# Series of unread matmuls behind the last output of a convolution network

## The chip, the cores and the metric

The kernel runs on one core of one Trainium2 chip. The metric is the device time of one execution in microseconds, the median of the runs shown. A profile of one execution gives the span from its first to its last instruction.

## The reference

The input is `x`, four images of 32 x 32 pixels with 16 channels, float32. Four residual layers follow one another: `x = x + layer(group_norm(x))`. Layers 0, 1 and 3 have the form

```python
first   = einsum('ijyx,byxc->bijc', M, x)
shifted = conv3x3(x, kernels)            # 32*32*16 output channels: one 3x3 filter per (i, j, f)
diff    = relu(x[:, None, None] - shifted)
second  = einsum('ijyx,bijyxc->bijc', W, diff)
layer   = first - second
```

so for every output pixel (i, j) and filter f the whole image is convolved with a filter of its own, subtracted, clipped and summed with weights W. Layer 2 pools over intervals and has three small dense steps with maxima. The result has the shape of `x`.

## The kernel before, in words

**Tiling.** The four images are two groups of two (`GB` = 2). Six phases run over (layer, group) for the three convolution layers; each phase has 8 tiles `t` of 128 output pixels, and each tile 32 steps (filter f of 16, image b of 2). That makes 1536 steps. A step makes, for 128 output pixels, the clipped and weighted sum over one image of 1024 pixels for one filter.

**A step on TensorE.** The image is cut into two halves of 512 pixels. The 9 taps x 16 channels of the contraction are spread over slots of 64 partitions: `iy`, `iz`, `iyz` have two slots each (`s` = 0, 1), `im9` one. To keep precision, each operand is split into an upper and a lower part; `WU`, `WL`, `WD` are the three weight parts (in one tile, `parts`, [128, 2, 3, 4, 128]), `W9` the weights of the ninth tap. `products` (line 593) issues, for each pair (weights, moving operand), two matmuls: one with partitions 0 to 63, one with 64 to 127, each into its own PSUM bank of a pair of banks, `half = h ^ b`. A step has 7 such pairs: 4 in `first_part` (line 610: `WU` x `iy` and `WL` x `iz`), then ScalarE scales the PSUM pair (line 630), then 3 in `second_part` (line 633: `WD` x `iyz` and `W9` x `im9`). The moving operand has `NH` = 512 columns, but the last matmul of the bank `half` = 1 has `LAST` = 480. All of them are recorded under line 601. At the end of a step VectorE reads the PSUM pair, clips it and multiplies with W, summing (line 646).

**Order of the work.** `conv_layer` (line 673) runs by hand: each step issues its `first_part`, then the `second_part` of the step before it, so that TensorE has work while ScalarE scales. Between steps, generators feed in small pieces of other work: the weights' preparation (`prep_parts`, line 213), the next phase's normalisation and images, the interval layer (matmuls of lines 521 and 534) and the first terms (matmuls of line 398: 256 moving columns, 32 weight columns, plain float32, which the profile shows as two records for each matmul). PSUM has four buffers, each a pair of banks (`bank_pair`, line 81), taken in rotation; a step's buffer is free when VectorE has read it.

**The end.** After the last phase the remaining `second_part` is issued (line 871): 3 pairs of matmuls, then VectorE's sum and the addition to `X` (line 664). The last line, 872, sends the last tile of `X` out by SyncE's queue. Nothing stands behind it.

Of the kernel before, what the change touches and what calls it, by code (L numbers as in the profile page):

```python
# [15 lines left out]
P = 128  # L16
B, H, C = 4, 32, 16
NG = 2
GB = B // NG
# [8 lines left out]
NH = HI * H  # L28
RUN = (HI - 1) * HP + H
LAST = (HI - 1) * H  # L30
ROWS = P // H
FU = 4
NU = C // FU
# [9 lines left out]
def net_kernel(ctx: ExitStack, tc: tile.TileContext, x, xq, xi, convs, iv_w, iv_b, out):  # L43
# [26 lines left out]
    nc = tc.nc  # L70
# [13 lines left out]
    def bank(name):  # L84
        return bank_pair(name)[:, 0]
# [3 lines left out]
    n_chunks = len(phases) * NT  # L89
# [12 lines left out]
    raws, units, chunks = {}, {}, {}  # L102

    def load_raw(u):
        if u < n_chunks * NU:
            n = u // NU
            raws[u] = wpool.tile([P, 3, FU, P], F32, tag="raw", bufs=RAWS, name=f"raw_{u}")
            nc.sync.dma_start(raws[u], convs[phases[n // NT][1]][2][n % NT, u % NU])
# [13 lines left out]
    iy = [const.tile([P, 2, GB, NH], F32R, name=f"iy{g}") for g in range(NG)]  # L122
    iz = [const.tile([P, 2, GB, NH], F32R, name=f"iz{g}") for g in range(NG)]
    iyz = [const.tile([P, 2, GB, NH], F32R, name=f"iyz{g}") for g in range(NG)]
    im9 = [const.tile([P, GB, NH], F32R, name=f"im9{g}") for g in range(NG)]
# [35 lines left out]
    pick = (ident[:, 4 * C : 5 * C], ident[:, :C])  # L161
# [9 lines left out]
    def halve(dst, src, mask):  # L171
        nc.scalar.activation(dst, src, AF.Copy, scale=mask[:, 1:2])  # L172
# [19 lines left out]
    def upper(src, n, name):  # L192

        t = work.tile([P, 2, NH], F32, tag="upper", bufs=2, name=f"upper_{name}")[:, :n]
        t = t.rearrange("p s (y x) -> p s y x", x=src.shape[3])
        nc.vector.tensor_scalar(  # L196
            t.bitcast(I32), src.bitcast(I32), HIGH, None, op0=ALU.bitwise_and
        )
        return t.rearrange("p s y x -> p s (y x)")

    def prep(u, at=0, to=FU, eng=nc.gpsimd):

        if u >= n_chunks * NU:
            return
        f0 = u % NU * FU
        for s in range(2 if u < PLAIN else 1):
            eng.tensor_tensor(  # L207
                raws[u][:, s, at:to], raws[u][:, s, at:to],
                pick[s][:, f0 + at : f0 + to].unsqueeze(2).to_broadcast([P, to - at, P]),
                ALU.subtract,  # L210
            )

    def prep_parts():

        for u in range(PLAIN, n_chunks * NU):
            parts = wpool.tile([P, 2, 3, FU, P], F32R, tag="parts", bufs=AHEAD + 1, name=f"parts_{u}")
            W9 = wpool.tile([P, FU, P], F32R, tag="W9", bufs=AHEAD + 1, name=f"W9_{u}")  # L220
            units[u] = [parts[:, :, k] for k in range(3)] + [W9]
            src = raws.pop(u)
            w8 = src[:, 0].rearrange("p f k -> p (f k)")
            WU, WL, WD = (parts[:, 0, k].rearrange("p f k -> p (f k)") for k in range(3))
            high = upper(src[:, 0:1], 1, f"w{u}")[:, 0]
            yield (IDLE,)
            halve(W9, src[:, 1], low_w)
            yield ()
            nc.scalar.activation(WD, high, AF.Copy, scale=-EPS)  # L229
            nc.gpsimd.tensor_tensor(WL, w8, high, ALU.subtract)  # L230
            nc.gpsimd.tensor_tensor(W9, W9.bitcast(F32), src[:, 2], ALU.add)  # L231
            yield ()
            nc.scalar.copy(WU, high)  # L233
            nc.gpsimd.tensor_tensor(WD, WD.bitcast(F32), WL.bitcast(F32), ALU.add)  # L234
            yield ()
            prep(u + 1)
            yield (IDLE,)
            yield (IDLE, CALM)
            for h in range(2):
                nc.sync.dma_start(  # L240
                    parts[64 * h : 64 * h + 64, 1].bitcast(F32),
                    parts[64 - 64 * h : 128 - 64 * h, 0].bitcast(F32),
                )
            load_raw(u + RAWS)
            yield (IDLE, CALM)
            yield (IDLE, CALM)
# [168 lines left out]
    wv = const.tile([P, 7, C], F32, name="wv")  # L415
# [308 lines left out]
    pairs = const.tile([P, C // 2], F32, name="pairs")  # L724
# [41 lines left out]
    def first_stats(src, name):  # L766

        ps = bank(f"ps_{name}")
        by_batch = work.tile([P, GB], F32, tag="by_batch", name=f"by_batch_{name}")
        nc.vector.tensor_scalar_mul(by_batch, own, src)  # L770
        nc.tensor.matmul(  # L771
            ps[:, :GB], lhsT=to_rows.rearrange("p k g s -> p (k g s)"), rhs=by_batch,
            start=True, stop=True,
        )
        return ps[:, :GB]

    nc.vector.tensor_reduce(s1, XQ, axis=AX.X, op=ALU.add)
    ps = bank("ps_own")
# [3 lines left out]
    m = first_stats(s1, "m0")  # L782
# [57 lines left out]
    def rest_of_start():  # L840
# [25 lines left out]
        yield from group_norm(0, "c00", xns[0], 4)  # L866

    parts = prep_parts()
    for phase in range(len(phases)):
        conv_layer(phase, behind(phase))  # L870
    second_part(*open_steps.pop(0))
    nc.sync.dma_start(out[1][:, NT - 1], X[1][:, NT - 1])


# [74 lines left out]
```

## Time and profile before

| | us |
|---|---|
| median of 2 runs (2525.25 and 2526.16) | 2525.7 |
| profiled execution, its own time | 2525.65 |
| its span | 2523.9 |
| TensorE busy | 2509.2, 21906 records |
| line 646 on VectorE | 1879.7, 1536 of 1.224 |
| line 630 on ScalarE | 1531.8, 1520 of 1.008 |
| start of the last pair of matmuls | 2519.22 |
| issue of the last DMA (line 872) | 2521.19 |
| that DMA from issue to landing | 1.4 |

How to read it: PE is TensorE's matmuls, PEld its weight loads, which are recorded apart and run beside matmuls. A record such as `64*128 64x512` is 64 rows of weights with 128 columns, and 64 partitions of 512 moving columns. In the timeline neighbouring records of one kind are merged; the first number is the start, the second the length of the merged piece, `x4` the number of records. A matmul's record lasts from its start to its modelled end, longer than the time after which the next can start.

### The profile page before, as it was taken

How to read it: one execution, taken by the hardware profiler on the slowest of the kernel's cores; microseconds unless marked ns; L12 is line 12 of the kernel's file. 1: busy time of each engine (PE TensorE's matmuls, PEld its weight loads, DVE VectorE, ACT ScalarE, POOL GpSimd, SP SyncE). 2: the span in 40 equal slices, each digit the busy share in tenths (PEclk: the TensorE clock that was granted, in tenths of full speed). 3: DMA queues.
4: the chain of work that ended last, by engine and by line, in shares of the span. 5: the costliest groups of instructions: out<-in, count | busy, mean ns of one | idle time of the engine just before them, and what ended most of it. 6: DMA issues, size and time to landing. Idle time of an engine off the chain costs nothing.

```text
span 2523.9 us, 56662 instructions
## 1 busy us (share of the span) xinstructions
PE 2509.2 (99%) x21906; PEld 2186.7 (87%) x21906; DVE 2080.3 (82%) x3621; ACT 1890.2 (75%) x2181; POOL 1103.6 (44%) x990
## 2 busy tenths in 40 slices
PE   8999999999999999999999999999999999999999
PEld 5888888888888888888888889988999898888887
DVE  8888777888777887777788988888888887778877
ACT  3777777787777777777777777787777777777776
POOL 3445333454333335333345555454646344333332
PEclk9999999999999999999999999999999999999999
DMA  5556444464444654444454444554444466354442
GB/s 173 180 151 169 120 135 137 117 168 139 131 139 131 200 163 118 139 131 133 135 143 134 131 119 136 144 159 128 124 135 137 130 170 201 111 143 134 134 135 53
DMA packets 81182, 353.80 MB, mean 140 GB/s; under 512 B 18448, under 2 KB 20368, under 8 KB 80144
## 3 DMA queue, kind: packets, MB, share of 16 engines
q1 hardware_dynamic: 79920, 349.57, 49.2%
q8 instruction: 172, 2.82, 0.5%
q14 instruction: 98, 0.80, 0.1%
q10 hardware_dynamic: 864, 0.58, 0.1%
q0 software_dynamic: 128, 0.02, 0.0%
HBM read 199.19 MB, written 0.98 MB: 79 GB/s over the span
## 4 chain that ended last, share of the span: by engine, by line
PE 99%; ACT 0%; DVE 0%; issue 0%; POOL 0%; DVEq 0%; ACTq 0%; POOLq 0%
PE pc L601 97%; PE pf L398 1%; ACT pc L630 0%; DVE junk L646 0%; PE ps_l L521 0%; PE ps_r L534 0%; ACT L326 0%; ACT L564 0%; DVE raw L817 0%; PE ps_y L585 0%; DVE kept L761 0%; DVE kept L757 0%; PE ps_v L771 0%; DVE raw L825 0%; DVE squares L794 0%
## 5 line engine op out<-in xcount | busy, mean ns | idle before, releaser
L646 DVE SCALAR_TENSOR_TENSOR junk<-pc,WT 128x1024 f32<-128x1024 f32 x1536 | 1879.7, 1224 | 419.0 <-PE pc L601 377.7
L630 ACT ACTIVATE pc<-pc 128x1024 f32<-128x1024 f32 x1520 | 1531.8, 1008 | 599.6 <-PE pc L601 566.5
L601 PE MATMUL pc<-iy,parts 64*128 64x512 f32 x6080 | 988.7, 393 | 0.1
L601 PE MATMUL pc<-iyz,parts 64*128 64x512 f32 x6080 | 971.8, 389 | 1.9 <-ACT pc L630 1.9
L601 PE MATMUL pc<-iz,parts 64*128 64x512 f32 x6080 | 968.3, 387 | 0.0
L601 PEld LDWEIGHTS pc<-iz,parts 64*128 64x128 f32 x6080 | 624.3, 184 | 85.7
L601 PEld LDWEIGHTS pc<-iyz,parts 64*128 64x128 f32 x6080 | 611.9, 184 | 89.1 <-ACT pc L630 5.8
L230 POOL TENSOR_TENSOR parts<-raw,upper_w 128x512 fp32r<-128x512 f32 x190 | 247.3, 1301 | 1008.6 <-PE pc L601 847.4
L601 PEld LDWEIGHTS pc<-iy,parts 64*128 64x128 f32 x6080 | 619.6, 184 | 78.2 <-issue 4.4
L601 PE MATMUL pc<-im,W 64*128 64x480 f32 (+1 forms) x3072 | 623.4, 384 | 0.0
L601 PEld LDWEIGHTS pc<-im,W 64*128 64x128 f32 x3072 | 311.4, 185 | 46.3 <-issue 3.4
L231 POOL TENSOR_TENSOR W<-W,raw 128x512 fp32r<-128x512 f32 x190 | 248.5, 1308 | 1.9 <-ACT W L172 1.6
L234 POOL TENSOR_TENSOR parts<-parts 128x512 fp32r<-128x512 f32 x190 | 247.8, 1304 | 2.7 <-ACT parts L229 2.5
L207 POOL TENSOR_TENSOR raw<-raw,ident 128x512 f32<-128x512 f32 x190 | 201.5, 1061 | 42.8 <-DMA raw<-in_g 34.8
L172 ACT ACTIVATE W<-raw,low_w 128x512 fp32r<-128x512 f32 x190 | 135.9, 715 | 0.1
L646 DVE DVE_READ_ACCUMULATOR junk<-pc,WT 128x1 f32 x1536 | 127.5, 83 | 0.0
L229 ACT ACTIVATE parts<-upper_w 128x512 fp32r<-128x512 f32 x190 | 118.5, 624 | 4.7 <-DVE upper_w L196 4.7
L233 ACT CAST parts<-upper_w 128x512 fp32r<-128x512 f32 x190 | 117.0, 616 | 0.0
L661 POOL TENSOR_SCALAR acc<-acc 128x32 f32<-128x32 f32 x40 | 11.5, 289 | 163.3 <-DVE junk L646 158.9
L196 DVE TENSOR_SCALAR upper_w<-raw 128x512 int32<-128x512 int32 x190 | 82.4, 433 | 0.2
L553 POOL TENSOR_TENSOR tables<-ft_b,rt 128x1089 f32<-128x1089 f32 x16 | 37.6, 2351 | 0.2
L553 POOL TENSOR_TENSOR tables<-ft_a,rt 128x1089 f32<-128x1089 f32 x16 | 37.7, 2355 | 0.0
(138 smaller groups left out, 397.3 us busy)
## 6 DMA issues: line engine op xcount, KB each, us to landing
raw<-in_g SPq DMA_DIRECT2D x190, 768.0 KB, 7.0
parts<-parts SPq DMA_DIRECT2D x380, 384.0 KB, 5.0
WT<-in_w SPq DMA_DIRECT2D x48, 512.0 KB, 4.7
MT<-in_mt SPq DMA_DIRECT2D x6, 2048.0 KB, 13.6
raw<-xs SPq DMA_DIRECT2D x120, 67.8 KB, 2.4
raw<-in_xi SPq DMA_DIRECT2D x3, 271.0 KB, 4.5
raw<-in_xi SPq DMA_DIRECT2D x1, 813.0 KB, 6.8
xs<-xt SPq DMA_DIRECT2D x20, 34.0 KB, 2.0
```

The costliest lines, as they stand in the source:

```text
L172: nc.scalar.activation(dst, src, AF.Copy, scale=mask[:, 1:2])
L196: nc.vector.tensor_scalar(t.bitcast(I32), src.bitcast(I32), HIGH, None, op0=ALU.bitwise_and)
L207: eng.tensor_tensor(raws[u][:, s, at:to], raws[u][:, s, at:to], pick[s][:, f0 + at : f0 + to].unsqueeze(2).to_broadcast([P, to - at, P]), ...
L229: nc.scalar.activation(WD, high, AF.Copy, scale=-EPS)
L230: nc.gpsimd.tensor_tensor(WL, w8, high, ALU.subtract)
L231: nc.gpsimd.tensor_tensor(W9, W9.bitcast(F32), src[:, 2], ALU.add)
L233: nc.scalar.copy(WU, high)
L234: nc.gpsimd.tensor_tensor(WD, WD.bitcast(F32), WL.bitcast(F32), ALU.add)
L553: nc.gpsimd.tensor_tensor(t, ft[:, i, :].unsqueeze(1).to_broadcast([P, T1, T1]), rt, ALU.add,)
L601: nc.tensor.matmul(ps[:, half, :n], lhsT=w[r], rhs=v[r] if n == NH else v[r][:, :n], start=first and k == 0, stop=k == len(pairs) - 1, ski ...
L630: nc.scalar.activation(ps, ps, AF.Copy, scale=1.0 + EPS)
L646: nc.vector.scalar_tensor_tensor(junk, ps.rearrange("p h n -> p (h n)"), 0.0, chunks[n], op0=ALU.min, op1=ALU.mult, accum_out=accs[phase][ ...
```

## The change

Behind line 872 the kernel issues further matmuls. None of their results is read, and `out` is not touched by them. Two helpers make them.

`more` takes a new PSUM pair and issues `count` rounds of one matmul on partitions 0 to 63 and one on 64 to 127 (`order`). Without arguments the weights are 128 columns of the last `parts` tile, another 128 in each round, and the moving operand is 512 columns of `iy[0]`, alternating between two places. Its arguments change one thing: `m` the weight columns, `n` the moving columns, `xc` and `wc` the pattern of the moving operand or the weights (counts and steps), `xo`, `wo` and `shift` where they start, `start=False` accumulation over all rounds, `order` the order of the halves, `x_all` the tile of the moving operand.

`replay` issues the matmuls of 8 steps (4 filters, 2 images), both parts of a step in a row, with the last weights and the second group's operands. `rest` is the column count of the last matmul on bank 1, and `pick` changes the list of pairs: `v` leaves out the seventh, `w` has the same weights for all seven pairs of a step, `x` the same moving operand, `y` the first two pairs three times, `z` six weights with one moving operand.

The only edit elsewhere keeps a reference to the last `parts` tile.

```diff
+    all_parts = [None]
...
             units[u] = [parts[:, :, k] for k in range(3)] + [W9]
+            all_parts[0] = parts
...
     nc.sync.dma_start(out[1][:, NT - 1], X[1][:, NT - 1])
 
+    xf = iy[0].rearrange("p s b n -> p (s b n)")
+    wf = all_parts[0].rearrange("p a k f n -> p (a k f n)")
+
+    last_unit = units[n_chunks * NU - 1]
+
+    def flat(v, count, step):
+        return bass.AP(v.tensor, v.offset, [list(v.ap[0])] + [[a, n] for n, a in zip(count, step)])
+
+    def more(name, n=NH, m=P, xo=0, wo=0, shift=0, xc=None, wc=None, start=True, swap=False, w_all=None, x_all=None, order=(0, 1), count=20):
+        ps = bank_pair(f"more_{name}_")
+        xv, wv = x_all if x_all is not None else xf, w_all if w_all is not None else wf
+        for k in range(count):
+            x0 = k % 2 * 512 + xo
+            w0 = k % 20 * 128 + wo
+            for h in order:
+                r = slice(64 * h, 64 * h + 64)
+                w = wv[r, w0 : w0 + m]
+                x = xv[r, x0 + shift * h : x0 + shift * h + n]
+                if wc:
+                    w = flat(w, *wc)
+                if xc:
+                    x = flat(x, *xc)
+                nc.tensor.matmul(
+                    ps[:m, h ^ (k % 2 if swap else 0), :n], lhsT=w, rhs=x,
+                    start=start or k < 1, stop=start or k == count - 1, skip_group_check=not start,
+                )
+
+    def replay(name, pick=None, rest=NH):
+        pair = [bank_pair(f"more_{name}{b}_") for b in range(GB)]
+        WU, WL, WD, W9 = last_unit
+        for f in range(FU):
+            for b in range(GB):
+                pairs = (
+                    [(WU[:, s, f], iy[1][:, s, b]) for s in range(2)]
+                    + [(WL[:, s, f], iz[1][:, s, b]) for s in range(2)]
+                    + [(WD[:, s, f], iyz[1][:, s, b]) for s in range(2)]
+                    + [(W9[:, f], im9[1][:, b])]
+                )
+                if pick:
+                    pairs = pick(pairs)
+                for k, (w, v) in enumerate(pairs):
+                    for h in range(2):
+                        r = slice(64 * h, 64 * h + 64)
+                        half = h ^ b
+                        n = rest if k == len(pairs) - 1 and half else NH
+                        nc.tensor.matmul(
+                            pair[b][:, half, :n], lhsT=w[r], rhs=v[r][:, :n],
+                            start=k == 0, stop=k == len(pairs) - 1, skip_group_check=True,
+                        )
+
+    hi = iyz[1].rearrange("p s b n -> p (s b n)")
+    more("a")
+    more("b", m=64)
+    more("c", m=32)
+    more("d", xc=((NH,), (0,)))
+    more("e", wc=((P,), (0,)))
+    more("f", xc=((2, 256), (256, 1)))
+    more("g", xc=((16, 32), (32, 1)))
+    more("h", xc=((NH,), (2,)))
+    more("i", wc=((P,), (2,)))
+    more("j", start=False)
+    more("k", shift=512)
+    more("m", n=448)
+    more("n", n=384)
+    more("o", n=496)
+    more("p", n=128)
+    more("q", wo=64)
+    more("wa", wo=8)
+    more("wb", wo=16)
+    more("wc", wo=32)
+    more("xa", xo=8)
+    more("xb", xo=16)
+    more("xc", xo=32)
+    more("xd", xo=64)
+    more("xw", xo=64, wo=64)
+    more("r", order=(0, 0, 1, 1), count=10)
+    more("s", x_all=hi)
+    replay("t")
+    replay("u", rest=LAST)
+    replay("v", pick=lambda p: p[:6])
+    replay("w", pick=lambda p: [(p[0][0], x) for w, x in p])
+    replay("x", pick=lambda p: [(w, p[0][1]) for w, x in p])
+    replay("y", pick=lambda p: p[:2] * 3)
+    replay("z", pick=lambda p: [(w, p[0][1]) for w, x in p[:6]])
```

## The prediction

> **What bounds the kernel now.** I read the page first (shares, granted clock, chain), then the rate of TensorE in a busy stretch and in the quiet last one, then single steps in the timeline, then the end of the timeline, because everything that is added stands behind the last matmul. The page:
>
> ```profile
> span 2523.9 us, 56662 instructions
> ...
> PE 2509.2 (99%) x21906; PEld 2186.7 (87%) x21906; DVE 2080.3 (82%) x3621; ACT 1890.2 (75%) x2181; POOL 1103.6 (44%) x990
> ...
> PEclk9999999999999999999999999999999999999999
> ...
> PE pc L601 97%; PE pf L398 1%; ACT pc L630 0%; DVE junk L646 0%; PE ps_l L521 0%; PE ps_r L534 0%; ACT L326 0%; ACT L564 0%; DVE raw L817 0%; PE ps_y L585 0%; DVE kept L761 0%; DVE kept L757 0%; PE ps_v L771 0%; DVE raw L825 0%; DVE squares L794 0%
> ```
>
> To see: the stream of line 601 is 97% of the chain that ended last, at full clock. So added matmuls of that kind have nothing to hide behind. The stretches by window:
>
> ```profile
> 2300.00:2400.00 100.00, 100.00 (x876) 87.04 (x874) 79.84 (x135) 75.85 (x87) 37.12 (x31) 1.00 0.48 136
> 2500.00:2517.00 17.00, 17.00 (x152) 14.76 (x150) 12.94 (x23) 11.05 (x11) 0.00 (x0) 1.00 0.01 2
> ```
>
> To see: 876 records in 100 us with GpSimd and DMA busy, 152 in 17 us with both idle. Some four records overlap the edges of a window, so it is 872/100 = 8.7 and 148/17 = 8.7 a microsecond: the rate doesn't depend on that traffic. Now two steps of the kernel, matmuls alone:
>
> ```profile
> 2500.42 0.63 PE L601 MATMUL pc<-iy,parts 64*128 64x512 f32 x4
> 2500.89 0.62 PE L601 MATMUL pc<-iz,parts 64*128 64x512 f32 x4
> 2501.34 0.63 PE L601 MATMUL pc<-iyz,parts 64*128 64x512 f32 x4
> 2501.80 0.40 PE L601 MATMUL pc<-im,W 64*128 64x480 f32 x2
> 2502.01 0.66 PE L601 MATMUL pc<-iy,parts 64*128 64x512 f32 x4
> 2502.48 0.64 PE L601 MATMUL pc<-iz,parts 64*128 64x512 f32 x4
> 2502.94 0.64 PE L601 MATMUL pc<-iyz,parts 64*128 64x512 f32 x4
> 2503.41 0.39 PE L601 MATMUL pc<-im,W 64*128 64x512 f32 x2
> 2503.63 0.40 PE L601 MATMUL pc<-iy,parts 64*128 64x512 f32 x2
> ```
>
> To see: matmuls go in pairs, one on partitions 0 to 63 and one on 64 to 127, side by side. From 2500.42 to 2503.63 are 3.21 us and 14 pairs. Each half has one matmul of 480 columns among its 14; 32 columns are some 0.014 us (0.23/512 each). A full pair is (3.21 + 0.014)/14 = **0.230 us**. The end:
>
> ```profile
> 2518.65 0.73 PE L601 MATMUL pc<-iyz,parts 64*128 64x512 f32 x4 [0.41 <-ACT pc L630]
> ...
> 2519.22 0.40 PE L601 MATMUL pc<-im,W 64*128 64x480 f32 x2
> ...
> 2520.97 0.19 DVE L664 SCALAR_TENSOR_TENSOR X<-acc,X 128x32 f32<-128x32 f32 x1
> 2521.19 0.35 SPq L872 DMA_DIRECT2D out<-X  x1
> ```
>
> To see: the last pair starts at 2519.22; then VectorE, the last DMA and the closing take until 2523.9. That tail runs beside the new stream.
>
> **The change part by part.** It removes and moves nothing; it issues no DMA, and no engine but TensorE gets work. The assignment that keeps the last weights tile emits no instruction.
>
> *How many.* 26 calls of `more`: 25 with 20 rounds of two matmuls, and r with 10 rounds of four, 40 matmuls = 20 pairs each. Seven calls of `replay`, 8 steps each: t, u, w, x have 7 pairs a step (56 each), v, y, z have 6 (48 each). Together 520 + 368 = 888 pairs.
>
> *Full pairs.* Twenty calls (a, d to k, q, the seven of wa, wb, wc, xa, xb, xc, xd, then xw, r, s; there is no l) have 128 weight columns and 512 moving columns: 400 pairs x 0.230 = 92.0. The replays are the same products in the same alternation: t, w, x, v, y, z are 312 pairs x 0.230 = 71.8; u has the kernel's own short halves: 56 pairs, 8 steps, four times the 3.21 us above = 12.8. Broken patterns (f, g): line 534 reads its moving operand in 11 runs of 32, two records of 352 columns, 0.75 us together and 454 ns each, so 0.30 us apart, 0.84 ns a column; line 398 reads 256 columns in one run in 0.217 us (next paragraph), 0.85 ns a column. No price shows; 0.230 kept.
>
> *Fewer weight columns* (b, c). The nearest row has 32-column weights:
>
> ```profile
> L398 PE MATMUL pf<-MT,xn 128*32 128x256 f32 x384 | 21.3, 380 | 0.0
> ```
>
> 384 records go in 96 groups of four side by side; each of the three layers' runs overhangs by about 0.16, so a group is (21.3 - 0.5)/96 = 0.217 us. A column there costs 0.85 ns, twice as much, so 256 of them are as long a stream as 512 here. Taken as the floor of a pair: 40 x 0.217 = 8.7. Other end: 0.230, +0.5.
>
> *Other lengths.* At 0.230/512 = 0.449 ns a column m (448) is 0.201, n (384) 0.172, o (496) 0.223: 20 x 0.596 = 11.9. For p (128 columns, 0.057) the weight load is the longer. Two loads on one half, one right behind the other, in the load queue's timeline:
>
> ```profile
> 1360.76 0.29 PEld L601 LDWEIGHTS pc<-iy,parts 64*128 64x128 f32 x2
> ```
>
> 0.29 less the 0.18 of one: 0.11 us apart. So p is 20 x 0.11 = 2.2, between 1.1 (streaming alone) and 4.6 (no gain over a full pair).
>
> *Strides and step zero* (d, e, h, i): no row has them. Ends: 0.217, if a repeated element spares something, and half rate for the moving side, 0.43, in h (+4.1) and less likely d. A weight load of doubled length, 0.22, would still fit beside a pair of 0.230, so e and i are at nothing, covered by the stream; without that cover they cost what is over 0.230. I take 0.230 for all four: each element is still read once. *Shifted starts* (k, q, wa to xw): operands at other addresses give 0.225 to 0.235 in the steps above (two pairs in 0.47, 0.45, 0.46), so +/- 1 us over 200 pairs; 0 taken.
>
> *Order 0,0,1,1* (r): one half's second matmul stands ahead of the other half's first. In the timeline the halves keep their own pace: behind the one-sided matmul of line 534 at 1358.95 an iz product starts at 1359.22 on one half, ahead of an iy one at 1359.38 on the other. Taken: 20 pairs x 0.230, in the full pairs above; other end 40 singles, +4.6. *Accumulating* (j): what line 601 does; 0. *Change of the array's split* before and after b and c: im at 247.47 to pf at 247.79 took 0.32 where a pair takes 0.23; three times 0.1 = 0.3.
>
> *Waits.* Each call reuses a PSUM pair; those of the first four had the last four steps' readers, of which only the last ends late (2520.94), and its pair goes to d, some 14 us on. From e on the earlier user is TensorE itself. Cost nothing; without that cover, 0.41 (the ACT wait above) per call, at most 13 us, and no reason for it.
>
> *Sum.* 92.0 + 71.8 + 12.8 + 8.7 + 11.9 + 2.2 + 0.3 = **199.7 us**. The first new pair can start at 2519.22 + 0.23 = 2519.45. The last starts 0.23 before 2719.15 and its record is 0.39 long: 2719.3. Closing: the last DMA, issued at 2521.19, lands 1.4 later (median of its line), at 2522.6, and the span ends 1.3 after that; with 1.3 the new span is 2720.6. The profiled execution was 2525.65 for a span of 2523.9, 1.75 around it: **2722.4 us**, +196.7. The median, 2525.7, is the same execution within 0.05.
>
> **Weighed against the Trainium skill.** The trace has 0.230 us per pair. "TensorE: Matmul & The Clock Gate", section "Back-to-back issue gap", gives N/2.4 + 2.5 ns for an isolated gap, 216 ns at 512, estimated from the page; its smaller streamed figure, 131 ns, is met by no row here, since even one half's matmul takes 0.230. By 216 the sum would be some 12 us lower, about 2711. The row decides. For h no row has a stride: "SBUF — State Buffer", section "Door 1: The DMA port swizzle", states that two hits in a 16-byte line keep full rate, which a step of two fp32 just gives; by it h is a plain pair.
>
> **The rivals.**
> A. *Special series cost more.* For: no row has a stride or the order 0,0,1,1. Against: independent halves. All ends together: r +4.6, h +4.1, p +2.4, b and c +0.5, shifts +1 = +12.6, about 2735.
> B. *The quiet stream runs at the floor*, 0.217 for all full pairs, the loads no longer in its way. For: VectorE and ScalarE fall silent. Against: no change of rate when GpSimd and DMA stopped. 400 + 368 + 60 = 828 pairs x 0.013 = -10.8: 2711.6.
> C. *The halves no longer run side by side*, or each call waits. 888 x 0.23 = 204 more: about 2926; with waits alone 2735. Against: replay t is line 601's own stream.
> D. *Not slower.* Results that nothing reads are dropped before the program is built, or most of it: then only the tail remains, 2525.7. The place is the 26 + 7 calls; it decides if under about 233 of 888 pairs stay (50.5 us for 2%, plus the 3.0 us that the old tail hides, by 0.230). For: nothing reads the tiles. Against: line 326 computes a spare value that no result depends on, and ACT L326 stands in the chain above, so unread work is emitted.
>
> **How the numbers follow.** Forecast 0.74, A 0.13, B 0.08, C 0.03, D 0.02. The likeliest case gives 2722.4, its own range 2714 to 2730. To leave out no more than C and D and tails, the range takes in A and B: 2710 to 2736. Two per cent is about what a measurement of this kernel can tell from no change. All but D are over 2%: slower 0.98, same 0.02, faster 0.
>
> **What would show it.** 40 matmul records per call, each call 4.6 us long (p 2.2, n 3.4, b and c 4.3), TensorE's chain to the very end, a granted clock of full speed. Wrong if r takes 9 us, h 8.6, p over 4, if replay t differs from 12.9, or if gaps with a releaser stand between calls.

## The result and the profile after

The changed kernel took 2724.4 us (two runs, 2724.31 and 2724.49) against 2525.7: ratio 1.0787, 95% interval 1.074 to 1.0833. The profiled execution is the one of 2724.31, with a span of 2722.6. From the page:

```profile
span 2722.6 us, 60214 instructions
...
PE 2711.1 (100%) x23682; PEld 2391.0 (88%) x23682; DVE 2080.7 (76%) x3621; ACT 1889.9 (69%) x2181; POOL 1104.0 (41%) x990
```

And a stretch among the new series, by window (length, then TensorE, weight loads, VectorE, ScalarE, GpSimd; granted clock, DMA share, GB/s):

```profile
2530.00:2630.00 100.00, 100.00 (x873) 87.48 (x871) 0.00 (x0) 0.00 (x0) 0.00 (x0) 1.00 0.00 1
```

To see: 1776 more TensorE records (888 pairs), no other engine with more work, and in the new stretch TensorE alone, without a gap, at full clock. The end of the old work, in the timeline of all engines:

```profile
2518.22 0.39 PE L604 MATMUL pc<-im,W 64*128 64x480 f32 x2
...
2518.44 4.73 PE L899 MATMUL more_a__31840<-iy,parts 64*128 64x512 f32 x40
...
2519.97 0.19 DVE L667 SCALAR_TENSOR_TENSOR X<-acc,X 128x32 f32<-128x32 f32 x1
2520.19 0.35 SPq L875 DMA_DIRECT2D out<-X  x1
```

The first series starts 0.22 us behind the last old pair, and VectorE's tail and the last DMA run beside it, as forecast. Single series, from the timeline of TensorE (a series lasts from its start to the next one's start; the lettered ones have 20 pairs each, t and u 56):

```profile
2522.98 4.79 PE L899 MATMUL more_b__31881<-iy,parts 64*64 64x512 f32 x40
2527.59 4.83 PE L899 MATMUL more_c__31922<-iy,parts 64*32 64x512 f32 x40
2532.24 4.50 PE L899 MATMUL more_d__31963<-iy,parts 64*128 64x512 f32 x40
2536.55 4.82 PE L899 MATMUL more_e__32004<-iy,parts 64*128 64x512 f32 x40
...
2550.26 9.25 PE L899 MATMUL more_h__32127<-iy,parts 64*128 64x512 f32 x40
2559.30 4.86 PE L899 MATMUL more_i__32168<-iy,parts 64*128 64x512 f32 x40
...
2628.85 4.72 PE L899 MATMUL more_r__32824<-iy,parts 64*128 64x512 f32 x40
2633.38 4.72 PE L899 MATMUL more_s__32865<-iyz,parts 64*128 64x512 f32 x40
2637.92 0.64 PE L922 MATMUL more_t__32906<-iy,parts 64*128 64x512 f32 x4
...
2650.61 0.64 PE L922 MATMUL more_u__33020<-iy,parts 64*128 64x512 f32 x4
...
2663.39 0.68 PE L922 MATMUL more_v__33134<-iy,parts 64*128 64x512 f32 x4
```

To see: h, with a step of two, takes 9.04 us (2559.30 - 2550.26) where r or s take 4.53. b takes 4.61: fewer weight columns don't make it shorter. d, which reads one element over and over, takes 4.31, 0.216 a pair. Replay t takes 12.69 (2650.61 - 2637.92) for 56 full pairs, **0.2267** each. Replay u, the same with 480 columns in eight of its matmuls, ends at 2663.39 where v starts: 12.78. It streams fewer columns and takes longer.

The sum by the prediction's own terms:

| term | forecast | measured |
|---|---|---|
| 20 series of full pairs | 92.0 | 96.0 (h 9.04, the other nineteen 87.0) |
| b, c | 8.7 | 9.26 |
| m, n, o | 11.9 | 12.0 |
| p | 2.2 | 2.2 |
| t, v to z | 71.8 | 70.8 |
| u | 12.8 | 12.8 |
| change of the array's split | 0.3 | within the above, none seen |
| start of the new stream | 2519.45 | 2518.44 |
| from its last record to the span's end | 1.3 | 1.0 |

So + 3.3 for the stream, - 1.0 for the old part (the runs of the kernel before spread over 3.2 us, 2524.57 to 2527.72), - 0.3 for the closing: 2722.4 became 2724.4.

### The profile page after: what moved, and what is told of

It is laid out like the page before. It is cut to its first block, busy times and chain, and to the rows that moved or that the text cites. A ratio compares the mean times of both kernels' runs of the same rounds, so it can differ in the third digit from the quotient of the medians.

```text
span 2722.6 us, 60214 instructions
## 1 busy us (share of the span) xinstructions
PE 2711.1 (100%) x23682; PEld 2391.0 (88%) x23682; DVE 2080.7 (76%) x3621; ACT 1889.9 (69%) x2181; POOL 1104.0 (41%) x990
## 4 chain that ended last, share of the span: by engine, by line
PE 98%; DMA 0%; ACT 0%; DVE 0%; issue 0%; ACTq 0%; DVEq 0%
PE pc L604 90%; PE pf L401 1%; PE more_h__32127 L899 0%; ACT pc L633 0%; DMA raw<-in_xi 0%; PE more_u__33021 L922 0%; PE more_x__33346 L922 0%; PE more_w__33232 L922 0%; PE more_t__32906 L922 0%; PE more_x__33347 L922 0%; PE more_w__33233 L922 0%; PE more_t__32907 L922 0%; PE more_u__33020 L922 0%; PE more_v__33134 L922 0%; PE more_z__33558 L922 0%
## 5 line engine op out<-in xcount | busy, mean ns | idle before, releaser
L604 PEld LDWEIGHTS pc<-iyz,parts 64*128 64x128 f32 x6080 | 620.2, 184 | 81.5 <-ACT pc L633 5.8
L604 PEld LDWEIGHTS pc<-iy,parts 64*128 64x128 f32 x6080 | 626.1, 184 | 70.8 <-issue 4.3
```

Of the source, the lines that this page charges most:

```text
L604: nc.tensor.matmul(ps[:, half, :n], lhsT=w[r], rhs=v[r] if n == NH else v[r][:, :n], start=first and k == 0, stop=k == len(pairs) - 1, ski ...
```

## The experiments

Two things needed a cause: h, and replay u. The second matters for the kernel itself, because u is what line 601 does in every step. First theory (A): the short matmul shifts the two halves against each other, and out of step they hinder each other. Rival (B): the columns alone set the time. A half is what runs on partitions 0 to 63, or on 64 to 127; its pace is the time from one of its matmuls' starts to the next. The trace doesn't name the half: starts are told apart by their order and spacing.

**All matmuls at 512.** The row that was skipped is set to zero for the first phase; in the later ones it comes from the padding.

```diff
-            n = LAST if k == len(pairs) - 1 and last and half else NH
+            n = NH
...
             eng.memset(v[:, :, H - 1 : H], 0.0)
+            eng.memset(v[64 - 64 * b : 128 - 64 * b, HI - 1, :], 0.0)
```

> The kernel before, without the appended series, with every matmul of line 601 at 512 columns (the 480 becomes 512 and the row it skipped is set to zero). Theory A, the halves fall out of step: the short matmul shifts one half against the other by 13 ns in every step, and pairs out of step take 0.230 us where replay t, with nothing short, took 0.2267. Then a step goes from 1.6035 to 7 x 0.2267 = 1.587, 1536 steps save 25 us: about 2500 us. Theory B, columns set the time: each half streams 32 columns more in every second step, 6.7 ns a step, plus 10 us: about 2536. Theory C, the last row of the step hides it: 2525.

Measured: 2504.4 us, ratio 0.9917 (0.9902 to 0.9931). More columns, less time. Two steps in TensorE's timeline:

```profile
2299.95 0.62 PE L601 MATMUL pc<-iy,parts 64*128 64x512 f32 x4
...
2301.31 0.39 PE L601 MATMUL pc<-im,W 64*128 64x512 f32 x2
...
2303.12 0.62 PE L601 MATMUL pc<-iy,parts 64*128 64x512 f32 x4
```

14 pairs in 3.17 us (3.21 before), 0.2267 each by the single starts. B is out. The size is near A's (21 us saved where 25 was expected), but near 1500 us the halves start 23 ns apart here and still keep 0.2267, and the next run too speaks against A's reason.

**480 columns on both halves.**

```diff
-            n = LAST if k == len(pairs) - 1 and last and half else NH
+            n = LAST if k == len(pairs) - 1 and last else NH
```

> The kernel before with 480 columns in the last matmul of both halves; it leaves out one image row of the ninth tap for the other half too, so part of the result is missing. Theory A (halves in step): 6 pairs of 0.2267 and one of 0.213, 1.573 a step, 30 ns less in 1536 steps: about 2479 us. Theory B (columns alone): 6.7 ns less a step, 2515. If the short matmul costs by itself: 2525 or more.

Measured: 2525.5 us, ratio 1.0000 (0.999 to 1.001). Neither A nor B: it is the third case, the short matmul costs by itself. Two steps in TensorE's timeline:

```profile
2299.69 0.63 PE L601 MATMUL pc<-iy,parts 64*128 64x512 f32 x4
...
2301.08 0.38 PE L601 MATMUL pc<-im,W 64*128 64x480 f32 x2
...
2302.89 0.63 PE L601 MATMUL pc<-iy,parts 64*128 64x512 f32 x4
```

3.20 us for 14 pairs. In the trace's records the halves here start 3 to 4 ns apart near 600, 1500 and 2300 us, and still one half's starts follow each other by 213 to 236 ns. The halves are in step and slow: A falls.

**Series h without its gaps.**

```diff
-    more("h", xc=((NH,), (2,)))
+    more("h")
```

> The changed kernel with series h reading its moving operand without gaps, like a. If the step of two alone made h 9.05 us instead of 4.54, the time falls by 4.5 us to 2719.9. If h's excess came from somewhere else in the stream (the series before or after), series h stays near 9 or the next one grows, and the time stays at 2724.4.

Measured: 2720.5 us (2720.16 to 2720.82), ratio 1.0773 (1.0757 to 1.0789), 3.9 less than the changed kernel. Its series h and i in TensorE's timeline:

```profile
2550.84 4.70 PE L899 MATMUL more_h__32127<-iy,parts 64*128 64x512 f32 x40
2555.37 4.83 PE L899 MATMUL more_i__32168<-iy,parts 64*128 64x512 f32 x40
```

h is 4.53 and i keeps its 4.7: the step of two alone made the 4.5 us; the rest of the difference is in the old part, which was 0.6 longer in this execution.

**A second list of series** behind the kernel before. Core of the edit: `more` with one half (`ba`, `bb`), all 128 partitions (`bc`), both operands shifted (`cb` to `cd`), weights shifted (`ce` to `cj`), lengths (`db` to `df`), one half set ahead (`ea`, `eb`), gaps (`fa` to `ff`, where `ff` reads each element twice), one element read over and over (`bd`, `ck`), weight columns (`ga` to `gc`), replays with 512, 496, 480 and 448 on one bank and with 480 on both.

```diff
-    more("a")
...
+    more("ba", order=(0,), count=30)
...
+    more("cc", xo=16, wo=16)
...
+    more("cg", wo=24)
...
+    more("fd", xc=((256, 2), (4, 1)))
+    more("fe", xc=((128, 4), (8, 1)))
+    more("ff", xc=((256, 2), (1, 0)))
...
+    replay("hb", rest=496)
```

> The kernel before with another list of series behind its last output (results unread). Theory A1, each weight load takes 32 cycles from the moving operand's stream of the same half: a pair in step takes (n + 32)/2.4 ns: 480: 213, 416: 187, 384: 173, 320: 147, 256: 120 (or 110 if loads bound). Theory A2, one cycle in 16 is lost to reading: 212, 184, 170, 142, 113. Rival, the two halves take it from each other: one half alone (ba, bb) then takes 216 a matmul, else 227; all 128 partitions in one matmul (bc) 227 by A, 216 by the rival. Weights and moving operand shifted alike (cb, cc, cd): 227 if only their distance counts, 233 if each start counts. Weights shifted by 4 to 56 columns: 232, unless one shift gives 216. Step zero with shifted weights (ck): 216. One half set ahead by 256 or 128 columns (ea, eb): back to 227 within some 12 pairs if the lag between the halves locks itself, 230 to 235 throughout if not. Gaps: 2, 3, 4 at 384 columns: 347 for all if a gap halves the rate, 347, 520, 690 if the distance counts; pairs of neighbours with gaps (fd) 227 if two elements are one read, 452 if not; runs of four with gaps (fe) the same; each element twice (ff) 216 to 222 if the line is kept. 96, 64, 32 weight columns: 225, 221, 219 by A1 if in step, 230 as in b and c if shorter loads fall out of step. Replay with 480 on one bank 228 a pair, with 480 on both banks 227 and 213.

Measured: 2782.2 us in a single run, which says little; what counts are the series. Four of them in TensorE's timeline (a record or two of a series can be merged elsewhere, where halves overlap):

```profile
2526.40 6.28 PE L901 MATMUL more_ba__31901<-iy,parts 64*128 64x512 f32 x27
...
2676.80 9.20 PE L901 MATMUL more_fd__33149<-iy,parts 64*128 64x512 f32 x39
2685.46 4.98 PE L901 MATMUL more_fe__33190<-iy,parts 64*128 64x512 f32 x39
...
2690.36 4.41 PE L901 MATMUL more_ff__33231<-iy,parts 64*128 64x512 f32 x38
```

What it showed, from the differences of neighbouring starts on one half:

- One half alone (`ba`): 27 records in 6.28, (6.28 - 0.39)/26 = 0.2265 us. The other half has no part in it. All 128 partitions in one matmul (`bc`) settle at 0.2267 as well. `ea` and `eb` settled at lags of 3 and 143 ns between the halves, both at 0.2267: **each half keeps a pace of its own**.
- Weights shifted by 4 to 56 columns: 229 to 234 ns a pair. Both operands shifted alike by 8, 16 or 32: 227. Only the **distance** of weights and moving operand counts. A distance of 64 columns (256 bytes) is as good as none: q and xd of the changed kernel, with one operand shifted by 64, settle at 227.
- An element read twice in a row (`ff`) or always (`bd`, `ck`, the latter with shifted weights): 216 ns. This points to the moving reads as the tight place: with half as many different elements read, a matmul takes 216, shifted or not.
- Gaps, at 384 columns: step 2, 3 and 4 take 340, 340 and 347 ns, against 173 without. Pairs of neighbours with gaps of two (`fd`) 451 at 512 columns, runs of four (`fe`) 233. So half rate for runs of one or two neighbours, with gaps of one, two or three elements alike, and nearly the full rate for runs of four; runs of three were not tried.
- 96, 64, 32 weight columns: 230, 230 and 232. A1's price for the loads (225, 221, 219) is refuted.

After a 480 on a half, its next matmuls start, in ns:

```
213, 235, 233, 236, 224, 231, 236, 228, 233, 231, 226, 227, ...   (replay with 480, one half)
220, 227, 226, 227, 227, ...                                      (replay with 496, one half)
```

The ten behind the short one are together 46 ns above 226.7; the short one saves 13. Net 33 ns, once per step and in turn on the two halves: 768 x 33 = 25 us for the kernel. In the traces the undisturbed starts of line 601 (under 245 ns on one half) are 228.7 ns apart on average in the kernel before and 226.5 in the repeated run with 512 (`e1_again`, below): some 24 us over 21140 starts on two halves, of which 21 to 22 reached the time. In the run with 480 on both halves a half has two short ones in 14; the second comes before the ten are over, and the excess is -27 + 59 = 32 in 14 matmuls, as much as before: that is why the time didn't move. Theory D, formed here: each half falls into an even pace of its own, and a matmul of 480 upsets it for ten matmuls while one of 496 doesn't.

**496 columns.** The line of `products` stays as before; with the zeroed row:

```diff
-LAST = (HI - 1) * H
+LAST = (HI - 1) * H + 16
```

> The kernel before with 496 columns in the matmul that had 480 (16 of the skipped columns are computed on zeros). Theory D, each half keeps a pace of its own that a matmul 32 columns shorter upsets for ten matmuls and one 16 shorter does not (replay with 496 in the probe: 220 ns, then 227 at once): per half and two steps 13 x 226.7 + 220 instead of 3207 as before or 3173 with 512, so 3.3 ns a step less than with 512, 5 us: about 2499, with 512 beside it at 2504. Rival, any short matmul upsets it: 2510 to 2525.

> All matmuls at 512 once more, beside the one with 496 on the same chip: 2504 as before by both theories.

Measured on one chip: 496 columns 2500.4 us (2499.02 to 2500.65; ratio 0.9897, 0.9881 to 0.9914), 512 columns 2503.5 (2503.23 to 2503.68; 0.9911, 0.9896 to 0.9926). Two steps with 496 in TensorE's timeline:

```profile
2299.70 0.65 PE L601 MATMUL pc<-iy,parts 64*128 64x512 f32 x4
...
2301.06 0.42 PE L601 MATMUL pc<-im,W 64*128 64x496 f32 x2
...
2302.86 0.65 PE L601 MATMUL pc<-iy,parts 64*128 64x512 f32 x4
```

3.16 us for 14 pairs: the saved columns are kept. 3.1 us less than with 512 where 5 was expected. Over the whole trace the undisturbed starts of line 601 (under 245 ns on one half) sum to some 5 us less than in the run with 512, and the longer ones, with waits and other matmuls between, to some 2 more. It is the fastest version here, 25 us below the kernel before.

**Moving operands 8 columns further on**, all matmuls at 512:

```diff
-    const.tile([P, 32], F32, name="pad")
+    const.tile([P, 40], F32, name="pad")
...
-    const.tile([P, 112], F32, name="pad_parts")
+    const.tile([P, 104], F32, name="pad_parts")
```

> All matmuls at 512, but the four moving operands start 8 columns (32 bytes) later in their partitions, by a filler 8 columns longer ahead of them and one 8 shorter behind; the weights stay. Theory E, the weight loads and the moving reads of one half disturb each other by the distance of their addresses (series with one of them shifted: 233 a pair, both shifted: 227): 6.6 ns more for each of 7 x 1536 pairs, 71 us: about 2575. Rival, the shift matters only in the bare series, or the seven operands' distances average out: 2504.

Measured: 2568.9 us (2568.61 to 2569.09), ratio 1.017 (1.0155 to 1.0185), 65 us above 2503.5. Two steps in TensorE's timeline:

```profile
2299.72 0.63 PE L601 MATMUL pc<-iy,parts 64*128 64x512 f32 x4
...
2302.98 0.63 PE L601 MATMUL pc<-iy,parts 64*128 64x512 f32 x4
```

3.26 us for 14 pairs, 0.233 each, as in the bare series. Thirty-two bytes of address decide over 65 us. Theory E's price for the distance, 71 us, holds in sign and nearly in size; the rival, that the shift doesn't matter in the kernel, is excluded. That it is the weight loads and the moving reads that disturb each other is not shown by this run.

**A third list** behind the kernel before: every fourteenth matmul short (`sa` 508, `sb` 504, `sc` 500, `sd` 496, `se` 492, `sf` 488, `sg` 480, on to `sn` 256), the same on one half, finer shifts, fewer weight columns at other shifts, more lengths.

```diff
-                x = xv[r, x0 + shift * h : x0 + shift * h + n]
+                c = short if short and k % 14 == 13 else n
+                x = xv[r, x0 + shift * h : x0 + shift * h + c]
...
+    more("sd", count=42, short=496)
...
+    more("sg", count=42, short=480)
```

> The kernel before with a third list of series behind its last output (results unread). Every fourteenth matmul short (508 down to 256 columns): theory D, a pace that repeats every 32 columns or a fraction of it: 496 costs nothing more, 480 loses 46 ns after it, others between; rival, the loss grows with the missing columns. The same on one half alone (tb, tc): the same steps if each half is by itself. Weights shifted by 1, 2, 4 and odd multiples of 4 columns: 230 to 235; a value under 226.7 would say that the present distance isn't the best one. Fewer weight columns at other shifts: 227 or below for one of them if only the distance spoils b and c, 230 for all if not. Constant lengths: (n + 32)/2.4 where a multiple of 64 is read, some ns more elsewhere.

Measured: 2868.4 us in a single run. Five of the series with short matmuls in TensorE's timeline:

```profile
2545.45 9.79 PE L902 MATMUL more_sc__32067<-iy,parts 64*128 64x512 f32 x84
2555.05 9.71 PE L902 MATMUL more_sd__32152<-iy,parts 64*128 64x512 f32 x84
2564.58 9.71 PE L902 MATMUL more_se__32237<-iy,parts 64*128 64x512 f32 x84
...
2583.69 9.80 PE L902 MATMUL more_sg__32407<-iy,parts 64*128 64x512 f32 x84
2593.31 9.78 PE L902 MATMUL more_sh__32492<-iy,parts 64*128 64x512 f32 x84
```

`sd` lasts 9.53 us (2564.58 - 2555.05) for 42 pairs with three short ones, `sc` with four columns more 9.60, `sg` with 480 9.62. A series ends on its third short matmul, so what follows that one falls into the next series: `sd` still holds the upset from `sc`. The single starts say more. Behind 496 a half goes on at 227 at once; behind 508 or 492 three starts of 231 to 233 follow, behind 500 five, behind 504, 488, 480, 472, 464 and 456 ten or so. The loss doesn't grow with the missing columns; no period of 32 columns shows either, for behind 448 it is four: both the period and its rival are out. On one half alone 480 is followed by the same starts. Shifts of the weights by 1, 2, 4 and so on up to 60 columns settle at 227 to 234; the 227 is that of 60 columns, and none is under 226.7. Fewer weight columns lie between 228 and 233 at every shift tried: the shift alone is not what spoils b and c. Constant lengths in ns a pair: 496 220, 464 210, 400 180, 384 173, 320 147, 256 120, 192 111 (about the loads' distance, 0.11 us). From 256 to 512 columns that is (226.7 - 120)/256 = 0.417 ns a column and 13.3 ns beside, A1's form; it fits the others from 256 to 496 within 3.3 ns, while 480, 448, 432 and 416 swing from pair to pair and lie 2 to 4 ns above it on the average. Being a multiple of 64 is not what decides: 448 is one and lies above, 496 and 400 are none and fit.

**What stays open**: by what the even pace comes about. Shown is that it belongs to one half, hangs on the distance of the weights' and the moving operand's addresses, costs some 13 ns per matmul, and all but vanishes when moving elements are read twice (216 ns, where 512 x 0.417 is 213.5). That it is a clash of the weight load's reads with the moving reads fits much of this, but fewer weight columns should then cost less, and they don't; nor does series e of the changed kernel, whose weight loads read one column over and over (0.232 a pair). Open too is why 496 upsets nothing while 508, 504, 500 and 492 do.

## Why the prediction was right, point by point

- *Count, place and cover* (888 pairs behind the last old one, the tail beside them, no waits between the calls): right; start 0.22 behind the last pair, no gap.
- *Full pair 0.230*: mis-sized. The two steps that it was taken from are upset by their own 480s; an even stream takes 0.2267. "Operands at other addresses give 0.225 to 0.235 in the steps" was the wrong reading of the spread: the same operands take 0.2267 throughout in t, so it was the pace. Cost: 1.0 us in t and v to z, where nothing was shifted; in the twenty series, those with shifted operands and those with weights read in steps (e, i) took 0.229 to 0.234 and hid most of it (the nineteen besides h: 87.0 where 87.4 was forecast).
- *u at the kernel's own rows*: right, 12.8, because those rows hold the upset.
- *Floor of 0.217 for b and c*: wrong, 0.231 and 0.232. The row of line 398 differs in more than the weight columns: its column takes 0.85 ns, so its moving reads have twice the time. In d and `ff`, with full loads, it is fewer moving reads that bring 0.216, so the short load is probably not what made that row fast; no run separates the two for line 398.
- *h at 0.230*: wrong, the largest miss (+ 4.4); "each element is still read once" doesn't hold the rate. The other end, 0.43 for half rate, was named (0.452 measured). Of rival A's terms those for h and for b and c came true, those for r and p didn't. By the prediction's own signs of being wrong, h failed (9.04, the sign was 8.6) and so, by little, did t (12.69, not 12.9).
- *e, i at nothing*: nearly, 0.232 and 0.234 a pair. *f, g, j, k* at 0.227, *r* at 0.227: no price, as argued; but f and g, though split into 2 and 16 pieces, read 512 neighbours without a gap, so they don't test broken patterns as the prediction calls them. The halves are even more by themselves than the one row of line 534 showed.
- *m, n, o and p*: right within 0.1; p goes by the loads' distance of 0.11.
- *Rival B* was out: silence of the other engines changed nothing (0.2267 in t and, with all engines at work, in the run with 512). *C and D* out.
- *The Trainium skill*: "TensorE: Matmul & The Clock Gate", section "Back-to-back issue gap", has some 216 ns for an isolated matmul of 512 columns; the runs show it where elements are read twice or always (d 4.31 us for 20), and 227 or more otherwise. "SBUF — State Buffer", section "Door 1: The DMA port swizzle", says that two hits in a 16-byte line keep full rate; `fd` and h, with two fp32 of each line, run at half rate, and only four in a row (`fe`) nearly reach it. The measurement decides against the page.

The total came within 2.0 us partly by luck: misses of + 4.4 (h) and + 0.6 (b, c) met - 1.4 (the pace), - 0.3 (no price for the array's split), - 1.0 (old part) and - 0.3 (closing).

## What to carry to other kernels

A rate averaged over a kernel's own steps can hold a disturbance that the kernel makes itself; replaying a step without one of its peculiarities shows it, and here led to 22 us less with 512 columns and 25 with 496. Where fp32r matmuls stream back to back, keep their lengths equal (or test which shortening is free), and keep the distance of weights and moving operand the one that runs best: 8 columns of shift cost 65 us here, and in the series shifts of 0, 60 and 64 columns were best. Read moving operands in runs of at least four fp32.

## What the runs showed of the hardware that I had not expected

- Dropping 32 columns from one matmul in fourteen of a half costs 33 ns net instead of saving 13; dropping 16 saves its 7.
- A matmul of fp32r with 512 columns takes 226.7 ns back to back at best, on 64 partitions alone or on all 128, and 216 only when its moving elements are each read twice or more.
- Step 2, 3 or 4 cost the same: 340, 340 and 347 ns at 384 columns.
- Halving or quartering the weight columns shortened the load records (184 to 131 and 105 ns) and lengthened the pair (0.2267 to 0.231 and 0.232).
